# A recurrent attention layer and a mixture of experts in one program: third-order roots, a state of 32-wide tiles, counts by doubling

## The chip, the cores and the metric

The program runs on one core of a Trainium2 chip. The metric is the device time of one execution in microseconds (us). All arithmetic is in 32-bit floating point. The engines are named as in the profile: PE (TensorE, matrix products into PSUM), DVE (VectorE), ACT (ScalarE), POOL (GpSimd) and SP (SyncE, which here only issues transfers).

## The reference, cut to what matters

The input x has 4 sequences of 1024 tokens with 256 channels. The first half is a linear attention with decay: after a layer norm, four mixtures of each token with its predecessor give r, k, v and g. There are 16 heads of 16 channels. In chunks, with w the decay of a head and Wmat the table of its powers:

```python
att = rc @ kc
yc = att * Wmat @ vc + rc @ state * wb
new_state = ws * state + kc * wk @ vc
```

The state of one head is a 16x16 matrix. y is normed per head (`(y - mean) / sqrt(var + EPS)`), scaled, gated by gelu(g), multiplied by Wo and added to x. The second half is a mixture of 8 experts (hidden size 896, two experts a token, at most 320 tokens an expert and sequence). A token's place among those of its expert is a running count over the tokens of the sequence. Tokens past the capacity are dropped; the rest go through `silu(h1) * h3` and w2, are weighted and added to x.

## The kernel before, in words

The sequence work runs in 16 blocks of 256 tokens (4 for each sequence), and each block in 2 chunks of 128 tokens. `front` makes the transposed input and the projections (`pc`, `pt`, `pk` are their PSUM banks). `chunk` computes the scores `pa` of the four groups of heads, multiplies them by the decay table on DVE (`aw`), adds up y in one PSUM bank and updates the state. `back` squares y, averages the squares per head on PE (`pv`), takes the inverse root on DVE (`rsqrt`, tiles `rah` and `ryh`), spreads it over the channels on PE (`prs`, two banks), scales and gates y on DVE (`ys`, `zT`), and multiplies by Wo (`po`); the product is added to x on DVE.

The state of 8 heads is kept as one 128x128 tile (`state`, two of them side by side). Only the 16x16 blocks on its diagonal are not zero: the products `pu` of keys and values are multiplied by a mask (`bd`) on DVE, giving `upd`, and POOL computes `state*ws + upd` in two instructions.

`rsqrt` takes an integer first guess and three Newton steps of three DVE instructions each. It is used on 128x128 tiles in `back`, and on 128x4 (or 128x2) tiles in `norm_stats`, the layer norms. It returns three parts, and `back` pauses (`yield`) after each of them. `route` chooses experts; its `before` tile holds, for each token tile, the sum of the choices of the tiles ahead of it, by one DVE addition a token tile (line 689).

The order on PE is written out by hand: for each block a list of 15 stages steps the generators of the current chunks `c[0]`, `c[1]`, of the fronts `f`, `fa` of the next blocks, and of `back`, which is called `new` in the block that it belongs to and `bk` in the next:

```python
(c[0], st), (f, st), (c[0], st), (bk, st), (f, bk, st), (c[0], bk, st), (c[1], fa, st), (f,), (fa,), (c[1],), (bk,), (f,), (c[1], fa, new), (f,), (bk,),
```

Between stages, matmuls of the experts of earlier sequences (`p`, `pw`) are put in by a credit of columns (`RATES`). So a step of `back` is moved in the PE order by the number of its pauses. The other engines' orders come from a scheduler. PSUM banks come from rings: four under the tag `m` (nearly all of `front`, `chunk`, `back`), one for y, three under `f` (experts, and in the first five blocks three of the four score banks). A bank of a ring is taken in turn and waits for the last reader of what it held.

## Time and profile before

| | us |
|---|---|
| median of 14 runs | 1020.4 |
| lowest and highest of them | 1015.9 and 1027.23 |
| the profiled execution | 1019.79 |
| its span (first to last instruction) | 1018.1 |
| PE busy in it | 955.3 |
| DVE busy | 499.0 |
| POOL busy | 266.2 |

In the profile a line of a group or of a timeline gives the source line (L481 is line 481), the engine, the operation, output and inputs by the program's names, shapes, and the count. One 32-bit matmul of the source shows as two MATMUL instructions. A form such as 128\*32 behind MATMUL gives the rows and columns of the array that the weights take. In a timeline the first column is the start in us from the span's start and the second is the time to the end; starts are records, ends of matmuls are modelled, so differences of starts are what is used here. The sequence work lasts from 9.6 us to about 634 us, the experts' matmuls fill in from about 129 us, and the rest of the span is experts alone.

### The profile page before, as it was taken

How to read it: one execution, taken by the hardware profiler on the slowest of the kernel's cores; microseconds unless marked ns; L12 is line 12 of the kernel's file. 1: busy time of each engine (PE TensorE's matmuls, PEld its weight loads, DVE VectorE, ACT ScalarE, POOL GpSimd, SP SyncE). 2: the span in 40 equal slices, each digit the busy share in tenths (PEclk: the TensorE clock that was granted, in tenths of full speed). 3: DMA queues.
4: the chain of work that ended last, by engine and by line, in shares of the span. 5: the costliest groups of instructions: out<-in, count | busy, mean ns of one | idle time of the engine just before them, and what ended most of it. 6: DMA issues, size and time to landing. Idle time of an engine off the chain costs nothing. (4 is left out here: it accounts for less than half of the span.)

```text
span 1018.1 us, 15797 instructions
## 1 busy us (share of the span) xinstructions
PE 955.3 (94%) x6046; PEld 762.0 (75%) x6046; DVE 499.0 (49%) x1484; ACT 259.1 (25%) x557; POOL 266.2 (26%) x268
## 2 busy tenths in 40 slices
PE   3999889989889899999999998999999999999996
PEld 2777678878777687888788787888876766866764
DVE  6898958677677545434653444522222222222221
ACT  4423425333433323132221311311111111101100
POOL 6232422521215501222145210271211111211111
PEclk9899999999999999999999999999999999999998
DMA  7992143534425524334446533675663245334421
GB/s 212 271 310 71 38 131 97 188 107 143 133 103 158 188 84 116 97 110 146 130 146 182 156 108 107 179 230 163 205 178 88 77 140 146 106 59 137 146 52 19
DMA packets 92068, 138.97 MB, mean 137 GB/s; under 512 B 5456, under 2 KB 73552, under 8 KB 91984
## 3 DMA queue, kind: packets, MB, share of 16 engines
q1 hardware_dynamic: 79120, 120.36, 36.6%
q0 software_dynamic: 12720, 17.47, 9.1%
q8 instruction: 52, 0.85, 0.3%
q14 instruction: 32, 0.26, 0.1%
q10 hardware_dynamic: 144, 0.02, 0.0%
HBM read 103.45 MB, written 34.39 MB: 135 GB/s over the span
## 5 line engine op out<-in xcount | busy, mean ns | idle before, releaser
L855 PE MATMUL p<-xeT,w 128*128 128x256 f32 (+2 forms) x1960 | 436.2, 376 | 10.8 <-ACT sl L860 4.2
L855 PEld LDWEIGHTS p<-xeT,w 128*128 128x128 f32 x1960 | 329.8, 193 | 101.1 <-issue 8.1
L847 DVE TENSOR_TENSOR act<-sl,p 128x256 f32<-128x256 f32 (+2 forms) x245 | 99.7, 407 | 262.6 <-PE p L855 250.1
L883 POOL DMA_INDIRECT y_out<-ye,xe x67 | 104.9, 1566 | 456.8 <-DVE ye L880 365.6
L876 PE MATMUL pw<-w,act 128*128 128x256 f32 x938 | 211.3, 381 | 0.7 <-ACT sl L860 0.5
L860 ACT ACTIVATE sl<-p 128x256 f32<-128x256 f32 (+2 forms) x245 | 91.7, 375 | 455.2 <-PE p L855 445.5
L876 PEld LDWEIGHTS pw<-w,act 128*128 128x128 f32 x938 | 175.7, 190 | 25.3 <-DVE act L847 0.8
L880 DVE TENSOR_SCALAR ye<-pw,xe 128x256 f32<-128x256 f32 x67 | 32.1, 482 | 121.4 <-PE pw L876 121.3
L469 DVE TENSOR_TENSOR aw<-pa,wmat 128x512 f32<-128x512 f32 x128 | 79.7, 681 | 9.6 <-PE pa L461 9.5
L758 POOL DMA_INDIRECT disp<-hs,is x64 | 64.0, 1000 | 41.6 <-issue 15.0
L386 PE MATMUL pc<-xm,wa 128*128 128x256 f32 x256 | 64.0, 396 | 9.7 <-DVE aw L469 6.6
L386 PEld LDWEIGHTS pc<-xm,wa 128*128 128x128 f32 x256 | 48.0, 195 | 21.3 <-DVE aw L469 9.2
L376 DVE SCALAR_TENSOR_TENSOR xm<-xx,ch,xT 128x256 f32<-128x256 f32 x96 | 48.7, 535 | 27.9 <-POOL xx L370 19.1
L513 POOL TENSOR_TENSOR state<-state,upd 128x256 f32<-128x256 f32 x24 | 17.7, 737 | 116.1 <-DVE upd L502 95.6
L461 PE MATMUL pa<-rT,kT 32*128 32x256 f32 x512 | 41.6, 403 | 0.8 <-DVE upd L502 0.2
L487 PE MATMUL y<-aw,vpad 128*32 128x128 f32 x1024 | 41.3, 278 | 0.2 <-DVE aw L469 0.2
L413 POOL TENSOR_TENSOR xm_g<-xx,ch 128x512 f32<-128x512 f32 x16 | 18.4, 1152 | 65.2 <-PE pc L386 55.6
L461 PEld LDWEIGHTS pa<-rT,kT 32*128 32x128 f32 x512 | 25.6, 184 | 11.9 <-issue 3.7
L562 PE MATMUL po<-wa,zT 128*128 128x256 f32 x128 | 31.6, 392 | 1.3 <-DVE zT L554 1.3
L423 PE MATMUL pt<-wa,xm 128*128 128x256 f32 x128 | 31.2, 386 | 1.5 <-DVE upd L502 0.9
L386 PE MATMUL pc<-xm_g,wa 128*128 128x256 f32 x128 | 32.1, 396 | 0.0
L487 PEld LDWEIGHTS y<-aw,vpad 128*32 128x32 f32 x1024 | 24.7, 109 | 8.6 <-issue 0.7
(168 smaller groups left out, 824.8 us busy)
## 6 DMA issues: line engine op xcount, KB each, us to landing
w<-w_in SPq DMA_DIRECT2D x96, 896.0 KB, 6.3
disp<-empty SPq DMA_DIRECT2D x8, 795.0 KB, 13.9
disp<-empty SPq DMA_DIRECT2D x16, 265.0 KB, 8.8
xe<-disp SPq DMA_DIRECT2D x16, 265.0 KB, 2.7
xe<-disp SPq DMA_DIRECT2D x8, 530.0 KB, 3.8
y_out<-x SPq DMA_DIRECT2D x8, 512.0 KB, 3.3
x<-x_in SPq DMA_DIRECT2D x7, 512.0 KB, 5.2
wa<-w_attn_in SPq DMA_DIRECT2D x5, 256.0 KB, 4.7
```

The costliest lines, as they stand in the source:

```text
L376: last["xm"] = nc.vector.scalar_tensor_tensor(xm[:, cc, :], xx[:, cc, :], maa(m, cc), xT[:, cc, 1:TB + 1], ALU.mult, ALU.add,).ins
L386: nc.tensor.matmul(pp[:, m * TB:(m + 1) * TB], wa[w][:, cc, m * P:(m + 1) * P], xm[:, cc, :], start=cc == 0, stop=cc == CC - 1,)
L461: nc.tensor.matmul(pa[g][:, cc * TB:(cc + 1) * TB], o.kT[rows32, cc, cols], o.rT[rows32, cc, :, cols], start=True, stop=True, tile_positio ...
L469: nc.vector.tensor_tensor(w.rearrange("p q i -> p (q i)"), pa[g], wmat[:, 4 * g:4 * g + 4, :].rearrange("p q i -> p (q i)"), ALU.mult,)
L487: nc.tensor.matmul(y[32 * g:32 * g + 32, :], o.vp[:, t, cc * 4 + g, q * 32:(q + 1) * 32], aw[g][:, cc * 2 + q, :], start=state is None and ...
L758: ins = nc.gpsimd.indirect_dma_start(out=disp[:, :], out_offset=bass.IndirectOffsetOnAxis(ap=idx_s[g][:, c, t:t + 1], axis=0), in_=last["h ...
L847: nc.vector.tensor_tensor(act, sl, p3[:, :w], ALU.mult)
L855: nc.tensor.matmul(pp[:, :w], wt[:, cc, f * P:(f + 1) * P], xeT[:, cc, lo:lo + w], start=cc == 0, stop=cc == CC - 1,)
L860: nc.scalar.activation(sl, p1[:, :w], AF.Silu)
L876: nc.tensor.matmul(po[:, :C], acts[f][:, i * P:(i + 1) * P], w2e[:, f, :], start=f == 0, stop=f == FC - 1,)
L880: nc.vector.tensor_scalar_mul(ye[:, i, :], po[:, :C], xe[:, t, C + 1 + e:C + 2 + e])
L883: ins = nc.gpsimd.indirect_dma_start(out=out[:, :], out_offset=bass.IndirectOffsetOnAxis(ap=xe.bitcast(I32)[:, t, C:C + 1], axis=0), in_=y ...
```

## The change

Three edits, all in one kernel.

The roots: `rsqrt` takes two steps of third order instead of three Newton steps; a step has four DVE instructions instead of three, and the argument is scaled by a constant in the instruction that adds epsilon. It returns two parts instead of three, so `back` has one pause less.

The state: it is kept for pairs of heads, as tiles of 32 rows and 32 columns, four above each other (so 128x64 in all instead of 128x256). Both the product with the state and the products of keys and values are issued as four small matmuls in place of one, and a mask of 2 columns (`par`) takes the place of `bd`.

The counts: the additions of line 689 become a few wide additions of doubled reach, in three constant tiles with zeros ahead.

```diff
+ROOT = (64.0 / 9.0) ** 2
...
+    sums = [const.tile([P, 4 + ST, E], F32, tag=f"sums{i}", name=f"sums{i}") for i in range(3)]
+    for t in sums:
+        nc.vector.memset(t[:, :4, :], 0.0)
...
             nc.vector.tensor_tensor(yi, magic_i.to_broadcast([P, n]), ai, ALU.subtract)
-            newton()
-        def newton():
-            nc.vector.scalar_tensor_tensor(a, y, -0.5, y, ALU.mult, ALU.mult)
+            step(1.0)
+        def step(scale):
+            nc.vector.scalar_tensor_tensor(a, y, scale, y, ALU.mult, ALU.mult)
             nc.vector.tensor_tensor(a, a, v, ALU.mult)
-            nc.vector.scalar_tensor_tensor(y, a, 1.5, y, ALU.add, ALU.mult)
-        return y, (guess, newton, newton)
+            nc.vector.scalar_tensor_tensor(a, a, -10.0 / 3.0, a, ALU.add, ALU.mult)
+            nc.vector.scalar_tensor_tensor(y, a, 5.0, y, ALU.add, ALU.mult)
+        return y, (guess, lambda: step(9.0 / 64.0))
...
             if state is not None:
-                nc.tensor.matmul(
-                    y, state[:, cc, :], o.rbT[:, cc, cols], start=True, stop=False,
-                    skip_group_check=True,
-                )
+                for g in range(4):
+                    rows32 = slice(32 * g, 32 * g + 32)
+                    nc.tensor.matmul(
+                        y[rows32, :], state[rows32, cc, :], o.rbT[rows32, cc, cols],
+                        start=True, stop=False, tile_position=(32 * g, 32 * g),
+                        skip_group_check=True,
+                    )
...
             for cc in range(CC):
-                nc.tensor.matmul(
-                    pu[:, cc * P:(cc + 1) * P], o.kw[:, t, cc * P:(cc + 1) * P],
-                    packed(o.vp, t, cc * 4, cc * 4 + 4), start=True, stop=True,
-                )
-            upd = sm.tile([P, CC, P], F32, tag="upd", name=f"upd{nm}", bufs=2)
+                for g in range(4):
+                    c0 = cc * P + 32 * g
+                    nc.tensor.matmul(
+                        pu[32 * g:32 * g + 32, cc * 32:cc * 32 + 32],
+                        o.kw[:, t, c0:c0 + 32],
+                        packed(o.vp, t, cc * 4 + g, cc * 4 + g + 1), start=True, stop=True,
+                        tile_position=(0, 32 * g), skip_group_check=True,
+                    )
+            upd = sm.tile([P, CC, 32], F32, tag="upd", name=f"upd{nm}", bufs=2)
...
-        nc.vector.tensor_scalar_add(var, pv[:, :P], GN_EPS)
+        nc.vector.tensor_scalar(var, pv[:, :P], GN_EPS, ROOT, ALU.add, ALU.mult)
...
+        k = 1
+        while 2 * k < nt:
+            src, dst = sums[k // 2], sums[k]
+            nc.vector.tensor_tensor(
+                dst[:, 4:4 + nt, :], src[:, 4:4 + nt, :], src[:, 4 - k:4 - k + nt, :], ALU.add)
+            k *= 2
+        src = sums[k // 2]
+        nc.vector.tensor_tensor(
+            earlier[:, 1:, :], src[:, 4:4 + nt, :], src[:, 4 - k:4 - k + nt, :], ALU.add)
+        if t0:
+            nc.vector.tensor_tensor(
+                earlier[:, 1:, :], earlier[:, 1:, :],
+                last["earlier"].unsqueeze(1).to_broadcast([P, nt, E]), ALU.add)
-        for t in range(nt):
-            nc.vector.tensor_tensor(
-                earlier[:, t + 1, :], earlier[:, t, :], mask[:, t, :], ALU.add
-            )
```

In the built programs the PE order of experts' matmuls, fronts and chunks is the same before and after, block by block. Of `back` two steps stand elsewhere: `prs` directly behind the `pu` of the next block's first chunk (before: behind that block's second scores `pa`, its `pt` and its `trx`), and `po` directly behind `trx` or the experts' work that follows it (before: behind the second chunk).

More of the change, by code (lines that the diff above doesn't have):

```diff
@@ L321, in norm_stats @@
             yield
-        nc.vector.tensor_scalar_add(ve, mv[:, :, 1], LN_EPS)
+        nc.vector.tensor_scalar(ve, mv[:, :, 1], LN_EPS, ROOT, ALU.add, ALU.mult)
         rs, parts = rsqrt(ve, n, nm)
@@ L326, in norm_stats @@
         parts[1]()
-        parts[2]()
         last["nb"] = nc.vector.scalar_tensor_tensor(
@@ L496, in chunk @@
             for cc in range(CC):
-                nc.tensor.matmul(
-                    pu[:, cc * P:(cc + 1) * P], o.kw[:, t, cc * P:(cc + 1) * P],
-                    packed(o.vp, t, cc * 4, cc * 4 + 4), start=True, stop=True,
-                )
-            upd = sm.tile([P, CC, P], F32, tag="upd", name=f"upd{nm}", bufs=2)
+                for g in range(4):
[7 more added lines that the diff above has]
+            upd = sm.tile([P, CC, 32], F32, tag="upd", name=f"upd{nm}", bufs=2)
             nc.vector.tensor_tensor(
-                upd.rearrange("p cc (h n) -> p cc h n", n=N),
-                pu[:, :C].rearrange("p (cc h n) -> p cc h n", cc=CC, n=N),
-                bd.unsqueeze(1).unsqueeze(3).to_broadcast([P, CC, HC, N]), ALU.mult,
+                upd.rearrange("p cc (q n) -> p cc q n", n=N),
+                pu[:, :CC * 32].rearrange("p (cc q n) -> p cc q n", cc=CC, n=N),
+                par.unsqueeze(1).unsqueeze(3).to_broadcast([P, CC, 2, N]), ALU.mult,
             )
@@ L509, in chunk @@
             else:
-                new = sm.tile([P, CC, P], F32, tag="state", name=f"state{nm}", bufs=2)
+                new = sm.tile([P, CC, 32], F32, tag="state", name=f"state{nm}", bufs=2)
                 nc.gpsimd.tensor_tensor(
-                    new, state, ws.unsqueeze(2).to_broadcast([P, CC, P]), ALU.mult)
+                    new, state, ws.unsqueeze(2).to_broadcast([P, CC, 32]), ALU.mult)
                 last["pool"] = nc.gpsimd.tensor_tensor(new, new, upd, ALU.add).ins
@@ L676, in route @@
         nc.vector.tensor_tensor(sel[:, 1], cand2, over_e(top2), ALU.is_equal)
-        mask = small("mask")
+        mask = sums[0][:, 4:4 + nt, :]
         nc.vector.tensor_tensor(mask, sel[:, 0], sel[:, 1], ALU.add)
```

## The prediction

> **What bounds the kernel now.** I read the page first, for which engine is full and where.

> ```profile
> span 1018.1 us, 15797 instructions
> PE 955.3 (94%) x6046; PEld 762.0 (75%) x6046; DVE 499.0 (49%) x1484; ACT 259.1 (25%) x557; POOL 266.2 (26%) x268
> ...
> PE   3999889989889899999999998999999999999996
> ...
> DVE  6898958677677545434653444522222222222221
> ```

> PE is busy in every slice but the first, and the last 16 slices, from about 634 us, are experts alone, which the change does not touch. But in slices 2 to 5 (25 to 127 us) DVE is at 80 to 90% too: there the two run nearly level, and either can be late. Second view, what PE waited for:

> ```profile
> PE pc L386 <- DVE aw L469: 6.6, 7, 1.6
> ...
> PE pcnt L694 <- DVE before L689: 2.5, 1, 2.5
> ...
> PE prs L546 <- DVE ryh L307: 1.3, 1, 1.3
> ...
> PE pt L423 <- DVE upd L502: 0.9, 1, 0.9
> ```

> The edits touch four things here: the state's matmuls on PE, the roots that `prs` waits for, `before`, and `upd`. PE waited 1.3 us in all for roots, in one of 16 blocks, and 2.5 us in all for counts. So shorter DVE work has little to win directly; what counts is PE's own time, and what the move of `prs` does. Third view, PE's timeline of one chunk, from the first product with the state:

> ```profile
> 181.03 0.38 PE L481 MATMUL y<-rbT,state 128*128 128x128 f32 x2
> 181.34 0.65 PE L487 MATMUL y<-aw,vpad 128*32 128x128 f32 x16
> 181.91 0.49 PE L481 MATMUL y<-rbT,state 128*128 128x128 f32 x2
> 182.33 0.64 PE L487 MATMUL y<-aw,vpad 128*32 128x128 f32 x16
> 182.91 0.71 PE L497 MATMUL pu<-vpad,kw 128*128 128x128 f32 x4
> 183.46 0.72 PE L855 MATMUL p<-xeT,w 128*128 128x128 f32 x5
> ```

> By starts the chunk takes 2.43 us: state 0.31, scores 0.57, state 0.42, scores 0.58, `pu` 0.55. Two full 128-column instructions follow each other in 0.11; one behind another shape of weights takes 0.20, and a second full one behind it 0.21. So each change of shape costs 0.09, and a return to full weights 0.10 more. Fourth view, the second block, PE and then DVE:

> ```profile
> 67.89 0.43 PE L531 MATMUL pv<-sq,avg 128*32 128x128 f32 x8
> ...
> 71.96 0.71 PE L497 MATMUL pu<-vpad,kw 128*128 128x128 f32 x4
> 72.60 1.15 PE L461 MATMUL pa<-rT,kT 32*128 32x256 f32 x16
> ...
> 76.04 1.06 PE L546 MATMUL prs<-ryh,spread 64*128 64x128 f32 x8
> ```
> ```profile
> 67.81 2.48 DVE L469 TENSOR_TENSOR aw<-pa,wmat 128x512 f32<-128x512 f32 x4
> ...
> 71.05 0.29 DVE L536 TENSOR_SCALAR var<-pv 128x128 f32<-128x128 f32 x1
> ...
> 75.45 0.28 DVE L307 SCALAR_TENSOR_TENSOR ryh<-rah,ryh 128x128 f32<-128x128 f32 x1
> ```

> The root is done at 75.73. `prs` stands at 76.04, so today it is just covered. Behind `pu`, at about 72.5, it is not.

> **The state on PE.** Per chunk each state product becomes 8 instructions on four 32x32 tiles. The nearest row for four tiles of 128 columns side by side is `pv`, 8 instructions: 67.89 to the next start at 68.25, 0.36 with the change of shape behind it; pairs, as in `prs`, take 0.65, one by one 8 x 0.11 = 0.87. I take 0.36, since the four tiles share neither rows nor columns. `pu` becomes 16 instructions with 32 moving columns. If weights of 32 columns load as fast as the pass of 40 columns in `pcnt` follows its forerunner (0.035 us), it is 4 x 0.035 + 0.20 to leave = 0.34; if each group of four costs what full weights cost, 4 x 0.11 + 0.14 = 0.58. I take 0.40, nearer to the short pass, because the weights are a quarter. `pu` now has the shape of the scores before it, so 0.09 falls away there. The sum: 0.09 to enter, 0.36 + 0.57 + 0.36 + 0.48 + 0.40, 0.10 for the first return to full weights: 2.36 against 2.43, -0.07 a chunk. With the ends of `pu` it is -0.13 to +0.11. No row shows a change between two small shapes without another wait; I take 0.09 for each of the three in a chunk, because every change that the trace does show cost it. If they are free, the chunk is at -0.34 to -0.40. Over 24 full chunks: -1.7 (-9.6 to +2.6). The four first chunks have `pu` alone (about -0.2 each), the four last the state alone (+0.07 each): -0.5. Together **-2.2**.

> [...]

> **DVE and POOL lighter.** A 128x128 root goes from nine instructions behind its guess (0.35, 0.34 and 0.31 each: 2.99) to eight (2.63): -0.36 x 16. `upd` goes from 0.42 to about 0.22, the row of `slot` from PSUM at 128x64: -0.2 x 28. Counts: 32 additions of 0.254 become 14 of about 0.22, -5.0. Layer-norm roots: one instruction of 0.17 less, 17 times. Three memsets of 0.07 are added ahead of the first norm, while DVE waits for x: nothing. In all DVE loses about 19 us of 499, 1.2 a block. State updates on POOL go from 0.74 and 0.61 to about 0.25, by the slope between 512 columns (1.15) and 256 (0.61): -20 us. POOL is on nobody's path but the state's, which has whole stages to spare, and DVE's: its roots stretch to 2.4 us beside POOL's additions. These feed the next two terms.

> **`prs` moves up.** With one pause less, it follows `pu` of the first chunk. I compare, block by block, the root's end (less 0.7: one instruction, and `upd`, which now stands behind it) with the end of those y matmuls plus 0.3 for `pu`. The trace gives root minus y of 2.3, 4.0, 3.1, 3.1, 0.1, 1.6 and 0.9 us for the first seven blocks. That makes waits of 1.3, 3.0, 2.1, 2.1, 0, 0.6 and 0 us. In the seventh an expert's product now stands earlier in DVE's order, before seven of the root's instructions of 0.32, which adds 1.4. From the eighth on y ends later than the root (0.1 to 4.6 us of slack); in the tenth an expert's product behind which the root waited leaves the chain. In the last block `prs` now precedes 3.0 us of experts that covered the root; they then cover the gating (a wait of 1.3 now): +0.6. Sum: 8.5 in the first four blocks and 2.6 later. Queued behind the wait on PE are `pa`, `pt`, `trx` and any experts.

> In the first four blocks this is given back in part: while PE waits, DVE catches up, and what PE waited for later is then ready. `pcnt` <- `before` (2.5) keeps about 0.5, `trx` waited 2.1 for a norm that DVE had mixed with scores, `pt` 0.9 for `upd`: -5.0. DVE's lists are 1.2 shorter in each of two blocks that started late: -2.4. `po`, 8 us earlier, also takes its addition and the next norm out of DVE's late queue. Net **+1.1** there; without this cover it would be +8.5.

> **Banks.** `prs` holds two of the four `m` banks just ahead of `pa`, which from the sixth block on wants all four. They come free after `ys`, `zT`, `ys`: 0.41 + 0.54 + 0.41 and a latency near 0.3 (`upd` starts that long behind the last `pu`), 1.7 us behind `prs`. Between stand one group of experts (0.9 and 0.1) or a transpose (0.55): I read waits of 0.3, 0.3, 0.35, 0.8 and 0.5 in blocks six to ten. From the eleventh on 3.5 us of experts lie between. **+2.3** (0 to +4.5, since `pt` behind it also waits for scores that now follow the gating on DVE). A shorter DVE list should take about one wait of `pc` <- `aw` (1.3) back.

> **Sum.** State -2.2, roots +1.1 and +2.6, banks +2.3, the wait of `pc` -1.3, and -1.2 for the stretched root instructions (about two of 0.6 us) that lighter POOL spares: +1.3. From the profiled execution, 1019.8 (1018.1 and 1.7 around it; 0.6 below the median), that gives **1021 us**: no change.

> **Rivals.** First, *small shapes follow each other freely*: three changes of 0.09 fall away in 24 chunks, -6.5, and with the short `pu` -8: 1013. For it: groups of the same shape already overlap their weights. Against: the 0.20 at every change seen. Second, *the wait for roots is not given back*: one place, `prs` behind `pu` in the first four blocks, 7.4 more than I count, 1028. It decides when DVE starts `var` over 2 us behind `pv`, as in blocks two and three now (3.2 and 3.1). Third, *the four state tiles do not run together*, all writing the bank of y: 0.87 in place of 0.36 twice a chunk, 28 chunks, +28.6: 1050. For it: the trace's row tiles (`pa`, `prs`) all write separate banks. Against: `pv`'s four write one. [...]

> **How the numbers follow.** My sum 0.54, its own range 1015 to 1027; the free shapes 0.25; the roots 0.13; the serial tiles 0.08. The range of 1009 to 1030 leaves out the serial tiles and the tails, about 2 in 10. A measurement tells 0.3%, 3.1 us, from none: faster 0.35 (most of the second case and a quarter of the first), the same 0.30, slower 0.35.

> **What would show it.** Right: a chunk of 2.3 to 2.4 us from state to `pu`'s end with starts 0.007 apart in a state group; PE waits for `ryh` of some 7 to 11 us; the wait for `before` nearly gone. Wrong: state groups 0.11 apart in single steps (third rival), 0.11 instead of 0.20 between state and scores (first), or PE waiting for `ryh` under 3 us.

## The result and the profile after

| | before | after |
|---|---|---|
| median, us | 1020.8 (47 runs) | 1035.2 (10 runs, 1031.75 to 1036.56) |
| ratio, 95% interval | | 1.0131 [1.0112, 1.0151] |
| profiled span | 1018.1 | 1030.5 |
| PE busy in it | 955.3 | 952.1 |
| PE idle in it (span less busy) | 62.8 | 78.4 |
| PE at half clock, without start and tail | 13.7 | 47.8 |

The change made the kernel 1.3% slower; 1035 us lies above the range that was forecast. The first lines of the page after:

```profile
PE 952.1 (92%) x6718; PEld 753.7 (73%) x6718; DVE 476.0 (46%) x1436; ACT 259.6 (25%) x557; POOL 248.7 (24%) x268
...
PE   3989888999888989999999998999999999999996
...
PEclk9999899999899879999999999999999999999998
```

and the granted clock before (PEclk, in tenths of full speed for each of 40 equal slices of the span):

```profile
PEclk9899999999999999999999999999999999999998
```

Three things are to be seen. DVE is 23 us lighter and POOL 17.5, near the 19 and 20 worked out. PE is lower than before in slices 3, 7, 13 and 15. And the granted clock, which the prediction never looked at, dips in slices 5, 11, 14 and 15. The profile's clock records give the stretches: 13.7 us at half clock before, in four pieces, 47.8 after, in nine, of which four lie between 75 and 144 us and four between 276 and 372.

What PE waited for after (total, times, longest), and then two of these waits before:

```profile
PE p L877 <- ACT sl L882: 10.8, 5, 4.6
PE prs L559 <- DVE ryh L314: 9.7, 3, 4.3
PE pe L849 <- DMA xe<-disp: 7.9, 3, 3.6
PE prs L559 <- DVE upd L515: 6.7, 4, 2.9
...
PE pa L467 <- ACT gT L455: 2.7, 2, 1.5
```
```profile
PE p L855 <- ACT sl L860: 4.2, 3, 2.5
...
PE pe L827 <- DMA xe<-disp: 3.3, 3, 1.4
```

`prs` waits 16.4 us in its two lines (before: 1.3). One line names `upd` as what ended the wait, but `prs` does not read it: in six of the seven waits `prs` starts 0.14 to 0.15 us after the end of the root (`ryh`), and in the last 0.05 us after it. Before, `p` waited 4.2 for `sl` and `pe` 3.3 for its load; now 10.8 and 7.9. `pa` waits 2.7 us behind `gT`, which it does not read either; `gT` is computed from a bank of the ring that `pa` takes its banks from, so this looks like a wait for a bank. Some waits are shorter: the 2.5 for `before` are gone, `trx` lost 2.4 of its 16.2 us, and `pc` 3.2 of the 6.6 for `aw`.

One chunk on PE, after:

```profile
350.19 0.42 PE L489 MATMUL y<-rbT,state 32*32 32x128 f32 x8
350.54 0.65 PE L496 MATMUL y<-aw,vpad 128*32 128x128 f32 x16
351.12 0.42 PE L489 MATMUL y<-rbT,state 32*32 32x128 f32 x8
351.47 0.64 PE L496 MATMUL y<-aw,vpad 128*32 128x128 f32 x16
351.93 0.31 PE L508 MATMUL pu<-vpad,kw 128*32 128x32 f32 x16
352.17 1.13 PE L392 MATMUL pc<-xm_g,wa 128*128 128x256 f32 x4
```

By starts: 0.35, 0.58, 0.35, 0.46, 0.24. In the records four state tiles start 0.007 us apart, and 0.20 passes from the last of them to the first score. So the third rival (serial tiles) and the first (free changes of shape) both fall, and the chunk is shorter than I worked out.

The second block on PE, behind the `pu` that starts at 71.70; then the window from 75.4 to 78.8 us (length, then busy time of PE, PEld, DVE, ACT and POOL, granted clock, DMA share, GB/s):

```profile
74.94 0.99 PE L559 MATMUL prs<-ryh,spread 64*128 64x128 f32 x8 [2.94 <-DVE upd L515]
75.86 2.09 PE L467 MATMUL pa<-rT,kT 32*128 32x256 f32 x16
77.88 2.36 PE L429 MATMUL pt<-wa,xm 128*128 128x256 f32 x8
```
```profile
75.40:78.80 3.40, 3.40 (x25) 2.26 (x23) 2.38 (x6) 0.00 (x0) 0.29 (x1) 0.52 0.71 275
```

Here is the whole story in one place. `prs` waits 2.9 us for the root, as forecast (3.0). Then the clock is halved for 3.4 us: from its start to that of `pt`, `pa` takes 2.02 us instead of the 1.08 that it took elsewhere at full clock. The wait is paid once as idle time and again as slow work behind it.

### The profile page after: what moved, and what is told of

Read it like the earlier page. It is cut to its first block, busy times and chain, and to the rows that moved or that the text cites. A ratio compares the mean times of both kernels' runs of the same rounds, so it can differ in the third digit from the quotient of the medians.

```text
span 1030.5 us, 17116 instructions
## 1 busy us (share of the span) xinstructions
PE 952.1 (92%) x6718; PEld 753.7 (73%) x6718; DVE 476.0 (46%) x1436; ACT 259.6 (25%) x557; POOL 248.7 (24%) x268
## 5 line engine op out<-in xcount | busy, mean ns | idle before, releaser
L877 PE MATMUL p<-xeT,w 128*128 128x256 f32 (+2 forms) x1960 | 437.5, 377 | 14.3 <-ACT sl L882 10.8
L475 DVE TENSOR_TENSOR aw<-pa,wmat 128x512 f32<-128x512 f32 x128 | 79.3, 682 | 18.4 <-PE pa L467 18.4
L382 DVE SCALAR_TENSOR_TENSOR xm<-xx,ch,xT 128x256 f32<-128x256 f32 x96 | 45.9, 510 | 38.8 <-POOL xx L376 29.3
L467 PE MATMUL pa<-rT,kT 32*128 32x256 f32 x512 | 44.1, 444 | 2.8 <-ACT gT L455 2.7
L526 POOL TENSOR_TENSOR state<-state,upd 128x64 f32<-128x64 f32 x24 | 8.3, 345 | 127.1 <-DVE upd L515 103.4
L467 PEld LDWEIGHTS pa<-rT,kT 32*128 32x128 f32 x512 | 27.0, 205 | 13.8 <-issue 4.6
L496 PEld LDWEIGHTS y<-aw,vpad 128*32 128x32 f32 x1024 | 24.6, 109 | 12.7 <-issue 11.2
L376 POOL TENSOR_TENSOR xx<-xT 128x512 f32<-128x512 f32 x16 | 19.0, 1189 | 59.6 <-ACT xT L373 59.6
L392 PE MATMUL pc<-xm_g,wa 128*128 128x256 f32 x128 | 32.6, 400 | 0.0
```

The source lines that it names most:

```text
L382: last["xm"] = nc.vector.scalar_tensor_tensor(xm[:, cc, :], xx[:, cc, :], maa(m, cc), xT[:, cc, 1:TB + 1], ALU.mult, ALU.add,).ins
L392: nc.tensor.matmul(pp[:, m * TB:(m + 1) * TB], wa[w][:, cc, m * P:(m + 1) * P], xm[:, cc, :], start=cc == 0, stop=cc == CC - 1,)
L467: nc.tensor.matmul(pa[g][:, cc * TB:(cc + 1) * TB], o.kT[rows32, cc, cols], o.rT[rows32, cc, :, cols], start=True, stop=True, tile_positio ...
L475: nc.vector.tensor_tensor(w.rearrange("p q i -> p (q i)"), pa[g], wmat[:, 4 * g:4 * g + 4, :].rearrange("p q i -> p (q i)"), ALU.mult,)
L496: nc.tensor.matmul(y[32 * g:32 * g + 32, :], o.vp[:, t, cc * 4 + g, q * 32:(q + 1) * 32], aw[g][:, cc * 2 + q, :], start=state is None and ...
L877: nc.tensor.matmul(pp[:, :w], wt[:, cc, f * P:(f + 1) * P], xeT[:, cc, lo:lo + w], start=cc == 0, stop=cc == CC - 1,)
```

## The experiments

My theory was that the move of `prs` and `po` is the loss while the arithmetic gains, and that a wait of PE costs more than its length because a half-clock stretch follows it. The rivals: the new shapes themselves cost, or a wait costs just its length. The expectations number their theories anew in each group of runs.

The first four kernels ran on one chip on which the kernel before took 1033.4 us, so their ratios to it count, not their times.

**Both steps back.** An empty part in the root puts `prs` and `po` where they were; all the arithmetic of the change stays.

```diff
-        return y, (guess, lambda: step(9.0 / 64.0))
+        return y, (guess, lambda: None, lambda: step(9.0 / 64.0))
...
+        parts[2]()
```

> The changed kernel with an empty third part of the root, so that `back` pauses as often as before and `prs` and `po` stand where they stood; roots, state tiles and counts stay as changed. Theory A (the loss is the moved step of `back`: PE waits for the roots, and half-clock windows that these waits bring): the gain of the chunks shows, about 0.26 us in each of 24, and some waits for DVE are shorter: 1010 to 1015 us, PE waits for `ryh` under 2 us, granted clock as before (0.98 to 0.99). Theory B (the small tiles or the new roots cost by themselves, through more instructions or DVE's order): 1030 us or more.

Measured: 1019.44 us, ratio 0.9881 [0.9838, 0.9925], a little more of a gain than the 1010 to 1015 us expected of a kernel that takes 1020.8. With the old order the same arithmetic is faster than the kernel before.

**The move alone.** The kernel before, with its two Newton steps in one part, so that one pause is gone.

```diff
-        return y, (guess, newton, newton)
+        return y, (guess, lambda: (newton(), newton()))
...
-        parts[2]()
```

> The kernel before with the two later Newton steps of the root in one part, so that `back` has one pause less; nothing else is changed. Theory A: the loss shows without any of the new arithmetic, and without the chunks' gain it is larger than the measured one: 1036 to 1045 us, with the granted clock at 0.97 or lower. Theory B: within 5 us of the kernel before.

Measured: 1049.78 us, ratio 1.0165 [1.0125, 1.0205]. `prs` waited 17.0 us in all and 44.4 us ran at half clock. The move alone makes the loss, without any new shape or root.

**The state alone.** The kernel before with the state's tiles of 32 rows and columns, `pu`, `upd` and POOL's update as in the change; roots and counts as before.

```diff
-                nc.tensor.matmul(y, state[:, cc, :], o.rbT[:, cc, cols], ...
+                for g in range(4):
+                    nc.tensor.matmul(y[rows32, :], state[rows32, cc, :], ...
...
-            upd = sm.tile([P, CC, P], F32, ...
+            upd = sm.tile([P, CC, 32], F32, ...
```

> The kernel before with the state tiles alone (32 rows and columns). Theory A: chunks of 2.17 us (state to return to full weights) in place of 2.43, less 6 us: 1012 to 1016 us. Theory B, if the tiles cost by themselves: 1025 us or more.

Measured: 1024.99 us, ratio 0.9908 [0.9876, 0.9941], by the ratio -9.5 us (-6.1 to -12.8). Nearly all of the gain of the arithmetic is here; roots and counts, the step from 0.9908 to 0.9881, lie within the two intervals.

**Useless work in the wait.** The changed kernel with three products of 128x512 ahead of `prs` in the first sequence's four blocks, where it waited 1.4, 2.9, 1.9 and 4.3 us.

```diff
+        for _ in range(3 if b == 0 else 0):
+            nc.tensor.matmul(pr[0], ident, wmat[:, 0:4, :]..., start=True, stop=True)
```

> The changed kernel with three needless full matmuls of 512 columns (2.6 us at full clock) ahead of `prs` in the first four blocks, into the bank that `prs` then overwrites. They do no useful work and fill the time in which PE waits for the root. If part of the loss is the clock that the waits bring (the half-clock windows at 75, 96 and 120 us in the changed kernel), those windows go and the time falls by 3 to 8 us although PE has 10 us more of work. If the loss is the waits alone, the time stays or grows by up to 4 us.

Measured: 1043.53 us, ratio 1.0085 [1.0053, 1.0116], by ratio 0.5% below the changed kernel, but not on its chip, and with half-clock stretches elsewhere that make 51.2 us in all; taken alone it settles nothing. The stretches near 75, 96 and 120 us are gone, as expected. What it shows is the second block, on PE:

```profile
72.64 2.84 PE L557 MATMUL prs<-wmat,ident 128*128 128x512 f32 x6
75.55 0.71 PE L563 MATMUL prs<-ryh,spread 64*128 64x128 f32 x8
76.19 1.15 PE L467 MATMUL pa<-rT,kT 32*128 32x256 f32 x16
77.27 1.99 PE L429 MATMUL pt<-wa,xm 128*128 128x256 f32 x8
79.10 0.60 PE L370 MATMUL trx<-ident,xn 128*128 128x128 f32 x4
```

`prs` to `trx` takes 3.55 us here, against 5.13 in the changed kernel (74.94 to 80.07): the same products are 1.58 us faster when PE was not idle ahead of them.

**Which of the two steps.** Four kernels on one chip (before: 1020.67). First the changed kernel once more.

> The changed kernel itself, to stand on one chip beside the three that follow. Both theories: 1.010 to 1.015 of the kernel before, as measured before, with 14 to 18 us of PE waiting for the roots ahead of prs, 9 to 12 us of p waiting for sl, and a granted clock of about 0.970.

Then `prs` early and `po` late, by one more pause ahead of `po`:

```diff
         yield
+        yield
         po = bank("m", f"po{nm}")
```

> The changed kernel with one more pause ahead of po: prs stays at its new place, po goes back behind the second chunk. Theory one (the wait for the roots ahead of prs is the whole loss): no change from the changed kernel, 1.010 to 1.015, since prs still waits 14 to 18 us. Theory two (the early po is the loss: it puts the next layer norm's work ahead of sl on ACT, and y_out, which waits for x, ahead of the xe loads on SP's queue): 0.988 to 0.992, as with both at their old places. Theory three, held likeliest, that both cost about half: 0.997 to 1.004, the waits of prs as in the changed kernel with their half-clock stretches before 130 us, but p's wait for sl down from 10.8 to 4 to 6 us, pe's wait for the load of xe from 7.9 to under 4, and the half-clock stretches at 277 and 359 us gone.

Then `po` early and `prs` late:

```diff
-        return y, (guess, lambda: step(9.0 / 64.0))
+        return y, (guess, lambda: None, lambda: step(9.0 / 64.0))
...
                 (bk,),
-                (f,),
+                (f, bk),
                 (c[1], fa, new),
                 (f,),
-                (bk,),
+                (),
```

> The other half of the move: all of the change's arithmetic, prs at its old place, po three stages earlier than in the kernel before (one stage later than in the changed kernel). Theory one (the wait for the roots is the whole loss): 0.986 to 0.990, prs waiting under 2 us. Theory two (the early po is the loss): 1.008 to 1.015, with p waiting 9 to 12 us for sl, SP's queue waiting 60 us or more for x, and half-clock stretches near 277 and 359 us. Theory three, each about half: 0.997 to 1.004.

And both late, with the edit of the first experiment:

> The changed kernel with an empty third part of the root, so that prs and po both stand where they stood before; measured once already, here on the same chip as the three others. All theories: 0.985 to 0.991, and a granted clock of 0.98 or more. Theory three adds that the loss of the two half moves over this kernel adds up to that of the changed kernel within 5 us.

Measured (span, busy and idle of the profiled executions; half clock without start and tail):

| | ratio, interval | median | span | PE busy | PE idle | half clock |
|---|---|---|---|---|---|---|
| changed kernel | 1.0127 [1.0085, 1.017] | 1035.24 | 1034.4 | 955.2 | 79.2 | 54.6 |
| only `prs` early | 1.0058 [1.0031, 1.0086] | 1028.17 | 1026.8 | 952.8 | 74.0 | 41.0 |
| only `po` early | 0.9995 [0.9974, 1.0016] | 1020.84 | 1021.6 | 953.9 | 67.7 | 27.3 |
| both back | 0.9874 [0.9831, 0.9918] | 1008.45 | 1005.6 | 944.8 | 60.8 | 13.7 |

These four have the same instructions on PE, 6718, so between them a difference of busy time is slower execution, not other work. From both back to the changed kernel the span grows by 28.8: 18.4 of idle time and 10.4 of slower execution. By medians the early `prs` costs 19.7 us (1028.17 less 1008.45) and the early `po`, on top of it, 7.1. The ratio with only `prs` early, 1.0058, is a little above the 0.997 to 1.004 expected if both cost about half: the early `prs` costs more. The waits of the kernel with `prs` early and `po` late:

```profile
PE prs L559 <- DVE ryh L314: 11.0, 4, 4.3
...
PE prs L559 <- DVE upd L515: 6.5, 4, 2.4
...
PE p L878 <- ACT sl L883: 6.3, 4, 2.5
...
PE pe L850 <- DMA xe<-disp: 3.2, 2, 1.6
```

The waits of `prs` stay, as expected, and those for `sl` and `xe` fall from 10.8 and 8.8 to 6.3 (just above the 4 to 6 expected) and 3.2: what is gone came from the early `po`. Not all that was expected came: half-clock stretches near 282 and 354 us remain. The longest wait for `sl` in the changed kernel, ahead of `p` at 279.17 us (4.58), reads on ACT:

```profile
275.02 0.60 ACT L343 ACTIVATE hs<-x,nbf,ryf 128x256 f32<-128x256 f32 x1 [2.68 <-DVE nbf L334]
275.64 1.28 ACT L455 ACT_TABLE_LOAD   x1
...
277.55 1.28 ACT L882 ACT_TABLE_LOAD   x1
278.84 0.45 ACT L882 ACTIVATE sl<-p 128x128 f32<-128x128 f32 x2
```

The same place with both steps back:

```profile
258.08 0.60 ACT L456 ACTIVATE gT<-pc 128x512 f32<-128x512 f32 x1
...
259.99 0.28 ACT L883 ACTIVATE sl<-p 128x128 f32<-128x128 f32 x1
...
268.08 1.09 ACT L344 ACTIVATE hs<-x,nbf,ryf 128x256 f32<-128x256 f32 x2 [4.86 <-DVE nbf L335]
```

With `po` early, the next norm's `hs` now stands ahead of `gT` and `sl`; ACT waits 2.68 us for its statistics, and two table loads of 1.28 us follow before `sl`, for which PE waits.

The kernel with only `po` early met the number expected of the theory that each step costs about half (0.9995), but not by the mechanism it named: `p` waited 6.8 us for `sl`, not 9 to 12, and SP's queue 22.5 for x, not 60. It paid for a wait of its own, since `po` there stands only one stage behind `prs`:

```profile
PE po L576 <- DVE zT L568: 10.3, 10, 1.6
```

So its 12.4 us over the kernel with both back are no measure of what the early `po` does to ACT and SP in the changed kernel; the 7.1 us are. The two halves, 19.7 and 12.4, add up to 5.3 us more than the 26.8 of both. How these 7.1 divide between ACT's order and SP's queue (which waited 73.1 us for x ahead of `y_out`, before 31.2) was not separated.

**The price of a wait by itself.** The kernel before, with 15 waits of known length on PE in the part where only experts run; then the same with useless products inside them (the loop over 3 is in the second kernel alone).

```diff
+        nc.tensor.matmul(ps1[:, :TB], ident, wf, start=True, stop=True)
+        nc.vector.tensor_tensor(af, ps1[:, :TB], wf, ALU.mult)
+        for _ in range(5):
+            nc.vector.scalar_tensor_tensor(af, af, 0.5, wf, ALU.mult, ALU.add)
+        for _ in range(3):
+            nc.tensor.matmul(ps2, ident, wmat[:, 0:4, :]..., start=True, stop=True)
+        nc.tensor.matmul(ps2[:, :P], ident, a[:, 0, :], start=True, stop=True)
```

> The kernel before with 15 waits of known length put on PE in the last 16 slices, where it runs experts alone: a marker product, six DVE instructions of 256 columns that start from it (0.42 and five of 0.48 us), and a product that needs their result. Each should hold PE idle for about 3.1 us and add 0.7 us of its own products. Theory one (a wait costs its own length): 15 x 3.8 = 57 us, a ratio of about 1.056. Theory two (a window of the clock with more than about 1.75 us of idle PE is followed by one at half clock, as all 62 such windows in the traces so far were): nine in ten of the waits bring a window of 3.41 us at half clock, up to 1.7 us each, 23 us more, a ratio of 1.070 to 1.080, and 12 to 15 half-clock windows between 640 and 1080 us.

> The same 15 waits, with three useless 128x512 products put between the marker and the product that waits: 2.9 us of work inside a wait of 3.1. Theory one: no faster than without them, a ratio of 1.056 or more, since PE does the same work and 43 us of useless work beside it. Theory two: 1.050 to 1.060 and 15 to 25 us faster than the kernel with bare waits, though it does more, with at most three half-clock windows between 640 and 1060 us.

Measured: bare waits 1097.13 us, 1.0729 [1.068, 1.0777]; filled 1077.63, 1.0538 [1.0497, 1.0578] (before: 1022.51). One of the 15 in each, bare and then filled (the marker product starts at 717.69 and 718.05):

```profile
721.10 0.72 PE L981 MATMUL stb<-stall,ident 128*128 128x128 f32 x2 [2.81 <-DVE stall L980]
721.61 1.06 PE L827 MATMUL pe<-ident,xe 128*128 128x128 f32 x4
722.47 5.77 PE L876 MATMUL pw<-w,act 128*128 128x256 f32 x21
```
```profile
718.49 2.74 PE L982 MATMUL stb<-wmat,ident 128*128 128x512 f32 x6
721.46 0.49 PE L985 MATMUL stb<-stall,ident 128*128 128x128 f32 x2 [0.24 <-DVE stall L980]
721.79 0.60 PE L827 MATMUL pe<-ident,xe 128*128 128x128 f32 x4
722.22 6.21 PE L876 MATMUL pw<-w,act 128*128 128x256 f32 x28
```

The bare one is followed by half clock from 721.2 to 724.6: its `pe` takes 0.86 us to the next start, the filled one's 0.43. The kernel that does some 40 us of useless work more is 19.5 us faster. Bare, the 15 waits of 2.9 us (43.3 in all) cost 74.6 us. PE's busy time grew by 32.6 us; the products around each wait take 0.77 us by the starts of the filled kernel (0.44 and 0.33), 11.6 in all, so some 21 us are slower execution, by this estimate. Ten half-clock windows lie between 720 and 965 us, two of them side by side (12 to 15 were expected), and with the filler there is none until the tail. A wait that costs just its length is refuted, and the clock is shown as the cause of the difference.

## Why the prediction was wrong

**The first step that failed: the sum had no term for the clock.** A wait was priced at its length. The half-clock stretches behind the waits added 10.4 us of slower execution between two orders of the same instructions, more than any net term of my sum. The granted clock of the kernel before was in its profile (0.986, with four half-clock stretches behind gaps) and was not used.

**The waits of `prs` were right in kind.** Forecast for the first four blocks: 1.3, 3.0, 2.1, 2.1; measured by the gap ahead of `prs`: 1.4, 2.9, 1.9, 4.3. Then 0, 0.6 and 1.4 were forecast for the fifth to seventh, and 0, 0.4 and 0 came. Missed were the fourth block (2.2 more) and the tenth (1.8, forecast as covered). In the last, 3.6 came; before, `prs` waited 1.3 there and `po` 1.3 for the gating, which is gone, so the net is +1.0 where 0.6 was forecast. Counted in this way the waits grew by 13.8 us, against 11.1.

**The give-back was there, in part for other reasons.** `before`, `trx`, `pt` and `pc` lost 9 us of waits, more than the 5.0 and 1.3 counted for them. But with both steps back the wait for `before` is gone already, so its 2.5 went with the shorter counts; and with only `prs` early `pc` keeps its 6.6, so its 3.2 went with `po`. Between these two kernels the waits of `prs` grow by 16.6 us (from 0.9 to 17.5) and PE's idle time by 13.2: at most 3.4, net, came back because PE waited. The 2.4 for shorter lists of DVE do not show: `prs` waited 10.5 us in the first four blocks, where 8.5 was forecast without them.

**The second step that failed: I took the early `po` as a gain for DVE's late queue.** It was a cost, 7.1 us: it reorders ACT and SP, and in the changed kernel `p` and `pe` wait 11.2 us more than before. I did not walk the early `po` past those two queues.

**The stretched root instructions.** The -1.2 for them did not come from lighter POOL. In the kernel before, the long ones (1.12 to 2.46 us) run beside the making of `xm_g` on POOL (lines 413 and 416), which the change leaves as it was; with both steps back, and lighter POOL, there are still six of 1.12 to 2.42 us.

**The state was mis-sized.** The chunk was worked out at 2.36 us. With the same 0.19 for entering and leaving, the starts above give 2.17, against 2.43 before: -0.26, or -6.2 over 24 chunks, where I had -1.7. Of the 0.19 between forecast and measurement, 0.16 is `pu`: 0.24, not 0.40, below my lower end of 0.34. Its groups of four start 0.03 us apart, as the short pass of `pcnt` did, and 0.13 passes from the last start to the next shape; the 0.20 that I took for leaving is that of a pass of 128 columns. The 9.5 us that the kernel with the state alone gained are 6.1 to 12.8 by its interval, so it is not shown whether anything came from elsewhere; POOL's additions to the state are shorter (0.35 for 0.74), but their part was not separated.

**Banks.** The waits of `pa` for banks that `prs` holds, counted at 2.3 us, do not appear. `pa` waits 2.7 us behind `gT` instead, and not at all with only `prs` early: this too goes with the early `po`.

**The rivals.** The second, waits not given back (1028), had the right side and the right place but not the whole mechanism: waits became shorter, though less of it than I thought by PE's waiting, and the clock and the early `po`, which it leaves out, took more. Serial tiles and free shapes are refuted by the starts 0.007 and 0.20 us apart.

In sums of the profiled executions: 12.4 us more of span are 15.6 more idle and 3.2 less busy. My terms for idle time (1.1, 2.6, 2.3, -1.3 and -1.2) came to 3.5; most of the 12.1 beyond them are the 11.2 of `p` and `pe`. The busy part, forecast at -2.2, looks right by luck: a gain of the arithmetic of 10.5 (the kernel with both steps back is that much less busy than the one before, with 13.7 us at half clock in each) is mostly eaten by slower execution (7.3).

## What to carry to other kernels

Price a wait on PE at its length and, if it leaves more than half of a 3.4 us window idle, add up to 1.7 us for the half-clock window behind it (84 of the 89 windows here with 1.70 us or more idle were followed by one). A pause that disappears from a hand-written order moves every later step of its generator: walk each of them past every engine and queue, and put the pause back if the slack was the point. Here the change with an empty pause in it is the fastest version measured, 0.9874 of the kernel before.

## What the runs showed of the hardware

In the changed kernel the four state tiles of a group differ in rows and columns, write one PSUM bank, and start 0.007 us apart; a group of eight takes 0.35 us to the next start, where the third rival put eight one by one at 0.87.
